# Loading x in half tiles from two queues, and making the edge keys later with one VectorE operation, in a graph attention kernel

## Chip, cores and metric

The kernel runs on one core of a Trainium2 chip. The metric is the device time of one execution in microseconds; lower is better. Where several executions were timed, the median is given.

## What is computed

A graph attention layer on 384 nodes with 1024 features, with a layer norm and a ReLU in front and a residual around it. Everything is float32. Cut to what matters:

```python
h = maximum(layernorm(x), 0)                      # x: [384, 1024]
q = h @ wq.T + bq;  k = h @ wk.T + bk;  v = h @ wv.T + bv
q2 = (q @ wiq.T + biq).reshape(384, 16, 64).transpose(1, 0, 2)      # k2, v2 alike
mask = full((384, 384), -inf)
mask[src, dst] = softplus(edge_type_weights)[edge_type - 1]         # 6528 edges
mask[i, i] = where(mask[i, i] == -inf, softplus(edge_type_weights)[3], mask[i, i])
attn = softmax(q2 @ k2.T * 0.125 + mask)
out = x + (attn @ v2).transpose(1, 0, 2).reshape(384, 1024) @ wo.T + bo
```

Edges can occur twice with different types, and then the last one counts. So the kernel must find out which edges have a later edge with the same cell of the mask.

## The kernel before, in words

**Precision.** Each float32 matrix is split in a high part, which TensorE's float32r format holds, and a low part, the remainder. A product is three matmuls, high by high, high by low and low by high (`mm3`, L367 to L369).

**Stages.** The weights are cut in 56 chunks of 128 x 1024 (512 KB each), in the order v, q, iv, k, iq and ik in turn, o. `load(w)` (L65) asks for chunk w from the queue of SyncE (SP) into one of three buffers `raw`; `split_hi` (L77, on ScalarE) and `split_lo` (L82, on VectorE or GpSimd) make the two parts, in one of four buffers `whl`. The first eight chunks give v from the normalized x, the next eight q, and so on; the attention over 16 heads runs between the chunks of iq and ik and those of o. The order on every engine is written out by hand, so an engine that waits for one instruction holds up all that stands behind it.

**The start**, where the change lies. x is loaded in three tiles `xt[0..2]` of 128 rows (L96). For each tile t:

- `ln_bn` (L251, VectorE, two halves) and `ln_mean` (L254, VectorE; for tiles 0 and 1 also L257 on ScalarE, minus the mean) make mean and variance.
- `ln_sub` subtracts the mean: for tiles 0 and 1 the first 512 columns on ScalarE (L280) and the others on GpSimd (L282), for tile 2 both on VectorE (L284).
- `ln_transpose` (L292, TensorE) turns the tile into two PSUM banks.
- `ln_hi` (L298, ScalarE) and `ln_lo` (L303, VectorE) read them, apply the ReLU, and write the high and the low part of `hT`.

The division by the standard deviation comes later, as a row that multiplies the product (`rrow`, L275), made from `ln_root` on ScalarE and `ln_rstd` on VectorE (L265 to L268).

Chunk 0 of the weights is split by GpSimd, in halves of 512 columns (L344 the high, L346 the low part). Its 24 matmuls (L414) stand in another order than those of the later chunks: eight with high parts alone, four with the low part of the weights, four with the low part of `hT` (k 0 to 3), and again four and four (k 4 to 7). So the low parts of `hT` are wanted in two steps. Chunk 1 is split on ScalarE and, by `split(1, nc.gpsimd)`, on GpSimd.

**The edge keys.** Every edge has a key, 384 times src plus dst. To compare an edge with later ones the kernel needs the keys twice: one edge to a partition (from `ed`), and as rows along the free axis in all partitions. The rows are made so: `er` (128 x 102 integers, 408 bytes a partition: src, then dst) is loaded, `key_rows` turns it into 128 x 51 keys `kr` on GpSimd (L182 to L184) and stores them to `krow` in DRAM (L185, SP), and `key_load` (L205, SP) reads `krow` back, spread over all partitions, into `rows`: three loads of 384 KB for group 0 at the start, others later. `mask_detect` (L217, VectorE) compares, from the end of chunk 0 on.

**Queues at the start.** SP issues, in this order: tile 0 of x, `er`, tiles 1 and 2, chunk 0, `ed`, chunk 1, `bc`, `ew` (small), the store of `krow`, chunk 2, three loads of `rows`, chunk 3. Chunk 3 waits for the buffer of chunk 0. ScalarE's queue issues no transfer there. While x is on its way, TensorE does transposes that nobody reads (`warm`, L309).

Of the kernel before, what the change touches and what calls it, by code (L numbers as in the profile page):

```python
# [12 lines left out]
OP = mybir.AluOpType  # L13

N, D, NT, KT, NP = 384, 1024, 3, 8, 8
E = 6528
EC = E // 128
# [5 lines left out]
def gnn_kernel(ctx: ExitStack, tc: tile.TileContext, x, edges, erows, etw, wq, wk, wv, wiq, wik, wiv, wo,  # L23
# [6 lines left out]
    nc = tc.nc  # L30
# [9 lines left out]
    NTAB, RNG = 3, EC // 3  # L40
# [3 lines left out]
    def bank(tag):  # L44
        return psum.tile([128, 512], F32, tag=tag, name=tag, bufs={"g": 3, "a": 1}.get(tag, 2))
# [14 lines left out]
    def load(w):  # L60
        if w >= NCH:
            return
        n, m = chunks[w]
        raw[w] = wpool.tile([128, D], F32, tag="raw", name="raw", bufs=3)
        nc.sync.dma_start(raw[w], W[n][m])  # L65
# [25 lines left out]
    xt = [xall[:, t * D:(t + 1) * D] for t in range(NT)]  # L91
    xn = [xall[:, (NT + t) * D:(NT + t + 1) * D] for t in range(NT)]
    ert = work.tile([128, N], F32, tag="e", name="er", bufs=EB)
    er = ert[:, :2 * EC].bitcast(I32)
    for t in range(NT):
        nc.sync.dma_start(xt[t], x[t * 128:(t + 1) * 128, :])  # L96
        if t == 0:
            nc.sync.dma_start(er, erows)
    load(0)
    ed = const.tile([128, 3 * EC], I32, name="ed")  # L100
    nc.sync.dma_start(ed, edges)
    load(1)
# [72 lines left out]
            nc.gpsimd.tensor_tensor(val, val, t, OP.add)  # L175

    krt = work.tile([128, N], F32, tag="e", name="kr", bufs=EB)
    kf = ert[:, :2 * EC]

    def key_rows():  # L180

        nc.gpsimd.tensor_copy(kf, er)  # L182
        nc.gpsimd.tensor_scalar(kf[:, :EC], kf[:, :EC], float(N), None, op0=OP.mult)
        nc.gpsimd.tensor_tensor(krt[:, :EC], kf[:, :EC], kf[:, EC:], OP.add)  # L184
        nc.sync.dma_start(krow.rearrange("c j -> (c j)").rearrange("(p e) -> p e", p=128), krt[:, :EC])  # L185

    rows = {}
# [3 lines left out]
    def parts(g):  # L191
        return [(r * RNG + g * PA, min(r * RNG + (g + 1) * PA, (r + 1) * RNG)) for r in range(NTAB)]
# [3 lines left out]
    def key_load(g, s):  # L196

        if s == 0:
            t = work.tile([128, 2, NT, N], F32R, tag="pt", name="rows")
            krv[g] = t.bitcast(F32).rearrange("p a k n -> p (a k n)")  # L200
        c0, c1 = parts(g)[s]
        dst = krv[g][:, s * PA * 128:(s * PA + c1 - c0) * 128]
        for c in range(c0, c1):
            rows[c] = krv[g][:, (s * PA + c - c0) * 128:(s * PA + c - c0 + 1) * 128]
        nc.sync.dma_start(dst, krow[c0:c1, :].rearrange("c j -> (c j)").partition_broadcast(128))  # L205
# [44 lines left out]
    def ln_bn(t, h):  # L250
        nc.vector.bn_stats(lnt[:, 30 + 12 * t + 6 * h:36 + 12 * t + 6 * h], xt[t][:, h * 512:(h + 1) * 512])  # L251
# [25 lines left out]
    def ln_sub(t, c0, c1, eng):  # L277
        src, dst = xt[t][:, c0:c1], xn[t][:, c0:c1]
        if eng is nc.scalar:
            nc.scalar.activation(dst, src, AF.Identity, bias=negm[:, t:t + 1])  # L280
        elif eng is nc.gpsimd:
            nc.gpsimd.tensor_tensor(dst, src, lnt[:, 2 * t:2 * t + 1].to_broadcast([128, c1 - c0]), OP.subtract)  # L282
        else:
            nc.vector.tensor_scalar(dst, src, lnt[:, 2 * t:2 * t + 1], None, op0=OP.subtract)  # L284

    def ln_transpose(t):
        pss = []
        for half in range(2):
            ps = bank("st"[half] if t < 2 else "ga"[half])
            for j in range(4):  # L290
                k = half * 4 + j
                nc.tensor.transpose(ps[:, j * 128:(j + 1) * 128], xn[t][:, k * 128:(k + 1) * 128], ident)  # L292
            pss.append(ps)
        return pss

    def ln_hi(t, half, ps):
        hi = hT[:, 0, half * 4:half * 4 + 4, t * 128:(t + 1) * 128]
        nc.scalar.activation(hi, ps.rearrange("p (k n) -> p k n", k=4), AF.Relu)  # L298
# [7 lines left out]
    def warm(n):  # L306
        for i in range(n):
            ps = bank("g")
            nc.tensor.transpose(ps[:, :128], ident, ident)  # L309

    mask_consts()
    warm(WARM[0])
    key_rows()
    load(2)
    for s in range(NTAB):
        key_load(0, s)
    ln_bn(0, 0)
    ln_bn(0, 1)
    ln_mean(0)
# [13 lines left out]
    ln_mean(2)  # L333
    ln_sub(2, 0, 512, nc.vector)
    ln_sub(2, 512, D, nc.vector)
    p1 = ln_transpose(1)
    warm(WARM[2])
    ln_hi(1, 0, p1[0])
# [6 lines left out]
    for c in (slice(0, 512), slice(512, D)):  # L345
        nc.gpsimd.tensor_tensor(t0[:, 1, c], raw[0][:, c], t0[:, 0, c].bitcast(F32), OP.subtract)  # L346
    load(3)
    ln_hi(2, 0, p2[0])
    ln_hi(2, 1, p2[1])
    ln_root()  # L350
# [416 lines left out]
    for i in range(S + LA + 4):  # L767
        now[0] = i
        r = RATE if len(gens) == 2 else RATE_O if i < S else RATE_E
# [86 lines left out]
```

## Time and profile before

| what | value |
|---|---|
| median of 3 runs | 302.65 us (302.16 to 302.67) |
| the profiled execution | 302.19 us, of which the span of the profile is 300.5 us |
| TensorE (PE) | 293.1 us busy, 98% of the span |
| VectorE (DVE), ScalarE (ACT), GpSimd (POOL) | 200.5, 154.9 and 155.7 us busy |
| DMA | 55.12 MB in 22,377 packets, mean 183 GB/s |
| PE's waits after 12 us | one, of 0.2 us |

How to read it: the profile shows one execution; a time is in us from the start of its span. A line of the timeline gives start, length, engine, line of the kernel, operation, what is written and read, how many instructions are merged, and in brackets the idle time before it with what ended it. `SPq` is the queue on which SP issues transfers; its lines show the issue, not the transfer. Tile names there can stand for several tiles in one buffer: `g` is x, `hT` and the like, and a PSUM bank too.

### The profile page before, as it was taken

What the parts mean: (1) busy time and instruction counts of PE and PEld (TensorE: products, weight loads), DVE (VectorE), ACT (ScalarE), POOL (GpSimd) and SP (SyncE); (2) the same over time, 40 slices, a digit from 0 to 9 for tenths busy, and PEclk for the clock granted to TensorE, in tenths of its full rate; (3) what the DMA queues carried; (4) which work ended last, traced back from release to release, by engine and by line L of the source; (5) the groups of instructions that cost most, each with busy time, mean ns of one, the idle gap of its engine ahead of it and who ended that gap; (6) DMA issues with size and microseconds to landing.
All of it is one profiled execution on the core that took longest, in us unless ns stands there. A gap on an engine that the chain in (4) does not pass through costs nothing.

```text
span 300.5 us, 4961 instructions
## 1 busy us (share of the span) xinstructions
PE 293.1 (98%) x1649; PEld 276.1 (92%) x1649; DVE 200.5 (67%) x492; ACT 154.9 (52%) x289; POOL 155.7 (52%) x164
## 2 busy tenths in 40 slices
PE   7899999999999999999999999999999999999995
PEld 5699999999988889999999999999999998888884
DVE  2959986655956463788865576767576757696523
ACT  3874644333422213554325667777777767676310
POOL 5865766271555785730033737373746467566210
PEclk9999999999999999999999999999999999999999
DMA  7899754642686668475369997646565636910005
GB/s 233 284 297 381 281 164 171 228 143 70 217 238 224 193 217 242 142 274 198 115 169 244 217 221 173 166 127 180 155 170 139 174 81 174 381 41 0 2 0 209
DMA packets 22377, 55.12 MB, mean 183 GB/s; under 512 B 4816, under 2 KB 8400, under 8 KB 22352
## 3 DMA queue, kind: packets, MB, share of 16 engines
q1 hardware_dynamic: 19968, 52.42, 57.7%
q0 software_dynamic: 2064, 1.80, 2.0%
q10 hardware_dynamic: 320, 0.59, 0.8%
q8 instruction: 13, 0.21, 0.3%
q14 instruction: 12, 0.10, 0.1%
HBM read 40.39 MB, written 4.97 MB: 151 GB/s over the span
## 4 chain that ended last, share of the span: by engine, by line
PE 95%; DMA 2%; DVE 1%; ACT 0%; issue 0%; SPq 0%
PE g L369 21%; PE g L367 21%; PE g L368 21%; PE s L694 6%; PE a L731 6%; PE t L714 5%; PE s L369 2%; PE s L368 2%; PE s L367 2%; DMA g<-in_x_dram 2%; PE t L369 2%; PE t L367 2%; PE t L368 2%; PE g L414 1%; PE a L369 1%; PE a L367 1%
## 5 line engine op out<-in xcount | busy, mean ns | idle before, releaser
L367 PE MATMUL g<-g,whl 128*128 128x384 f32 x312 | 106.4, 341 | 0.0
L369 PE MATMUL g<-g,whl 128*128 128x384 f32 x312 | 104.5, 335 | 0.0
L368 PE MATMUL g<-g,whl 128*128 128x384 f32 x312 | 104.2, 334 | 0.0
L228 POOL DMA_INDIRECT tab<-val,idx x51 | 57.6, 1129 | 40.3 <-issue 11.3
L77 ACT ACTIVATE whl<-raw 128x1024 fp32r<-128x1024 f32 x51 | 53.4, 1051 | 31.7 <-PE g L369 20.1
L709 POOL TENSOR_TENSOR e<-e,s 128x384 f32<-128x384 f32 x48 | 39.2, 830 | 41.2 <-DVE s L708 32.9
L368 PEld LDWEIGHTS g<-g,whl 128*128 128x128 f32 x312 | 58.7, 188 | 0.0
L367 PEld LDWEIGHTS g<-g,whl 128*128 128x128 f32 x312 | 58.6, 188 | 0.0
L369 PEld LDWEIGHTS g<-g,whl 128*128 128x128 f32 x312 | 58.5, 188 | 0.0
L82 DVE TENSOR_TENSOR whl<-raw,whl 128x1024 fp32r<-128x1024 f32 x41 | 50.2, 1224 | 9.6 <-ACT whl L77 7.9
L82 POOL TENSOR_TENSOR whl<-raw,whl 128x1024 fp32r<-128x1024 f32 x11 | 26.5, 2412 | 35.6 <-ACT whl L77 31.8
L383 ACT ACTIVATE g<-f,bc 128x384 fp32r<-128x384 f32 x24 | 14.8, 618 | 53.1 <-DVE f L382 46.8
L704 ACT ACTIVATE e<-e,s 128x384 f32<-128x384 f32 x48 | 29.4, 612 | 13.0 <-DVE s L700 13.0
L724 DVE TENSOR_TENSOR pt<-t,pt 128x384 fp32r<-128x384 f32 x48 | 26.4, 550 | 13.9 <-ACT pt L723 13.3
L723 ACT ACTIVATE pt<-t 128x384 fp32r<-128x384 f32 x48 | 23.2, 484 | 13.9 <-PE t L714 13.3
L700 DVE CUSTOM_DVE_ANT_0 e<-s,ma 128x384 f32<-128x384 f32 x48 | 26.3, 550 | 2.0 <-PE s L694 1.8
L694 PE MATMUL s<-ks,qs 128*128 128x384 f32 x96 | 25.3, 344 | 0.3 <-DVE s L700 0.2
L714 PE MATMUL t<-ident,e 128*128 128x128 f32 x144 | 23.5, 271 | 0.0
L382 DVE TENSOR_TENSOR f<-g,rrow 128x384 f32<-128x384 f32 x24 | 13.3, 555 | 13.5 <-PE g L369 7.6
L714 PEld LDWEIGHTS t<-ident,e 128*128 128x128 f32 x144 | 18.8, 140 | 3.1
L378 DVE SCALAR_TENSOR_TENSOR nat<-g,bc,nat 128x384 fp32r<-128x384 f32 x16 | 9.9, 618 | 16.4 <-ACT nat L377 14.4
L731 PE MATMUL a<-pt,vhl 128*128 128x384 f32 x96 | 20.8, 351 | 0.0
(147 smaller groups left out, 414.8 us busy)
## 6 DMA issues: line engine op xcount, KB each, us to landing
ks<-nat SPq DMA_DIRECT2D x30, 192.0 KB
raw<-in_wv_dram SPq DMA_DIRECT2D x8, 512.0 KB
raw<-in_wq_dram SPq DMA_DIRECT2D x8, 512.0 KB
raw<-in_wiv_dram SPq DMA_DIRECT2D x8, 512.0 KB
raw<-in_wk_dram SPq DMA_DIRECT2D x8, 512.0 KB
raw<-in_wiq_dram SPq DMA_DIRECT2D x8, 512.0 KB
raw<-in_wik_dram SPq DMA_DIRECT2D x8, 512.0 KB
raw<-in_wo_dram SPq DMA_DIRECT2D x8, 512.0 KB
```

The costliest lines, as they stand in the source:

```text
L77: nc.scalar.activation(dst[0], raw[w], AF.Copy)
L82: (eng or nc.vector).tensor_tensor(lo, raw[w], hi.bitcast(F32), OP.subtract)
L228: nc.gpsimd.indirect_dma_start(out=tabs[c // RNG], out_offset=bass.IndirectOffsetOnAxis(ap=idx[:, c:c + 1], axis=0), in_=val[:, c:c + 1], ...
L367: nc.tensor.matmul(ps, lhi, rhi, start=first, stop=False)
L368: nc.tensor.matmul(ps, lhi, rlo, start=False, stop=False)
L369: nc.tensor.matmul(ps, llo, rhi, start=False, stop=last)
L694: nc.tensor.matmul(ps[:, :N], qs[:, o, t * 128:(t + 1) * 128], ks[:, o, s, :], start=(s == 0), stop=(s == 1))
L704: nc.scalar.activation(es[i], es[i], AF.Exp, bias=s[:, 0:1], scale=-1.0, accum_out=s[:, 1:2])
L709: nc.gpsimd.tensor_tensor(es[i], es[i], s[:, 2:3].to_broadcast([128, N]), OP.mult)
L714: nc.tensor.transpose(ps[:, k * 128:(k + 1) * 128], es[i][:, k * 128:(k + 1) * 128], ident)
L724: nc.vector.tensor_tensor(lo, pv, hi.bitcast(F32), OP.subtract)
L731: nc.tensor.matmul(ps[:, :N], vhl[:, k, p, 2 * o:2 * o + 2, :], pts[h][:, s, k, :], start=(k == 0 and s == 0), stop=(k == 2 and s == 1))
```

## The change

Each tile of x is loaded in two pieces of 64 rows (256 KB each), the lower from SP's queue and the upper from ScalarE's. `er` is requested behind x and chunk 0 instead of behind tile 0. The keys are made by one VectorE operation (multiply by 384 and add, reading the integers directly) in place of three GpSimd operations. `key_rows`, with its store, stands behind the subtraction of tile 2 on VectorE and behind `load(2)` on SP; the three `key_load`s of group 0 stand behind `load(3)`.

```diff
     for t in range(NT):
-        nc.sync.dma_start(xt[t], x[t * 128:(t + 1) * 128, :])
-        if t == 0:
-            nc.sync.dma_start(er, erows)
+        for q, r in ((nc.sync, 0), (nc.scalar, 64)):
+            q.dma_start(xt[t][r:r + 64, :], x[t * 128 + r:t * 128 + r + 64, :])
     load(0)
+    nc.sync.dma_start(er, erows)
     ed = const.tile([128, 3 * EC], I32, name="ed")
...
     krt = work.tile([128, N], F32, tag="e", name="kr", bufs=EB)
-    kf = ert[:, :2 * EC]
 
     def key_rows():
 
-        nc.gpsimd.tensor_copy(kf, er)
-        nc.gpsimd.tensor_scalar(kf[:, :EC], kf[:, :EC], float(N), None, op0=OP.mult)
-        nc.gpsimd.tensor_tensor(krt[:, :EC], kf[:, :EC], kf[:, EC:], OP.add)
+        nc.vector.scalar_tensor_tensor(krt[:, :EC], er[:, :EC], float(N), er[:, EC:], op0=OP.mult, op1=OP.add)
         nc.sync.dma_start(krow.rearrange("c j -> (c j)").rearrange("(p e) -> p e", p=128), krt[:, :EC])
...
     mask_consts()
     warm(WARM[0])
-    key_rows()
     load(2)
-    for s in range(NTAB):
-        key_load(0, s)
     ln_bn(0, 0)
...
     ln_sub(2, 0, 512, nc.vector)
     ln_sub(2, 512, D, nc.vector)
+    key_rows()
     p1 = ln_transpose(1)
...
     load(3)
+    for s in range(NTAB):
+        key_load(0, s)
     ln_hi(2, 0, p2[0])
```

## The prediction, made before the change was run

> **What bounds the kernel now.** First the share of each engine: PE is busy for 293.1 of 300.5 us. So only a few us can be won without removing matmuls. Then the waits of PE: after 12 us it waits once, for 0.2 us. Then the chain of waits in order of time, from the start to the first weight matmul:
>
> ```profile
> 0.81 0.39 SPq L96
> 1.25 0.42 SPq L98
> 1.72 5.41 DMA g<-in_x_dram
> 7.16 1.30 DVE lnt L251 x2
> 8.96 0.73 ACT g L280
> 9.73 0.66 PE s L292 x4
> 10.39 0.45 PE t L292 x4
> 10.85 0.63 PE g L292 x4
> 11.51 0.66 PE a L292 x4
> 12.26 4.41 PE g L414 x24
> ```
>
> The reader is to see that PE's gapless work begins at 12.26 us, and that one transfer stands in front of it: the second tile of x, asked for at 1.72 us and awaited by VectorE until 7.16. VectorE had finished tile 0 at 5.69 (5.48 + 0.21), so it idled 1.47 us (the timeline says so). A shift of that landing shifts the start of PE, and, as nothing stops PE later, the end.
>
> Why was the tile late? I ask for busy time by stretches (last three columns: clock, DMA share, GB/s):
>
> ```profile
> 3.75:6.00 2.25, 2.21 (x11) 1.55 (x9) 1.50 (x3) 0.24 (x2) 1.19 (x4) 1.00 0.95 245
> 6.00:7.50 1.50, 0.77 (x7) 0.77 (x8) 0.34 (x1) 0.76 (x2) 0.81 (x1) 1.00 1.04 399
> ```
>
> From 3.75 to 6.00 the engines moved 551 KB; at 399 GB/s that takes 1.38 us, so 0.87 us were lost there, just where the 408-byte rows of `er` lie between tiles 0 and 1.
>
> The third view is the timeline of VectorE and GpSimd around the place where the new key operation goes:
>
> ```profile
> 11.14 2.72 POOL L346 TENSOR_TENSOR whl<-raw,whl 128x512 fp32r<-128x512 f32 x2
> 11.38 1.27 DVE L303 SCALAR_TENSOR_TENSOR g<-s,g 128x512 fp32r<-128x512 f32 x2
> ...
> 14.20 2.41 POOL L82 TENSOR_TENSOR whl<-raw,whl 128x1024 fp32r<-128x1024 f32 x1
> 14.37 0.68 DVE L303 SCALAR_TENSOR_TENSOR g<-a,g 128x512 fp32r<-128x512 f32 x1
> 14.96 0.16 DVE L265 RECIPROCAL lnt<-lnt 128x3 f32<-128x3 f32 x1
> 15.23 1.40 DVE L266 TENSOR_TENSOR lnt<-lnt 128x3 f32<-128x3 f32 x1
> 16.58 0.35 POOL L153 TENSOR_SCALAR ed<-ed 128x51 f32<-128x51 f32 x1
> 16.66 0.16 DVE L267 TENSOR_TENSOR lnt<-lnt 128x3 f32<-128x3 f32 x1
> ```
>
> L266 and L267 are alike, three columns each, yet one takes 1.40 us and the other 0.16: L266 ends at 16.63, with GpSimd's L82 (16.61).
>
> **What the Trainium skill says.** "SBUF — State Buffer", Who interferes with whom: a VectorE instruction with two SBUF inputs and a GpSimd instruction that reads SBUF exclude each other; the later one blocks until the earlier ends. L266 agrees (1.40 against 0.16). The new operation has two SBUF inputs; L303, which reads one from PSUM, runs in 0.68 beside L346. "DMA: Bandwidth & Descriptors", Issuing engines are not separate DMA queues: transfers from SP and ACT share the same 16 engines, and a second issuing engine saves issue time only. The trace before doesn't show x from two queues. So I expect nothing from the second queue by itself; SP's issues of x (0.39 to 0.43 us each) all end by 2.62, long before the landings.
>
> **The change part by part.** All times are of the profiled execution.
>
> *er behind x and chunk 0.* It frees tiles 1 and 2 of the 0.87 us at least. VectorE can't start tile 1 before 5.69, so the gain is between 0.87 (landing at 6.29) and 1.47 (5.69 or earlier). Tile 0 landed 3.35 us after its issue (0.81 to 4.16); 512 KB more at 399 GB/s take 1.31 us, which gives 5.47 for tile 1, and 6.8 for tile 2, needed at 7.2. I take a shift of **1.35 us**, nearer the upper end, because the loss in GB/s is a mean and the landing is that of the slowest of 16 engines.
>
> *Pieces of 64 rows, three issues on ACT.* Six issues for three. ACT starts at 0.80 and has a table load (1.28) and a root (0.20) before its first real work at 5.72: 5.72 - 0.80 - 1.50 = 3.4 us are free for three issues. At SP's price they take 1.3 us, hidden. The nearest ACT rows are dearer when both queues issue at once: 0.51 and 0.87 us (L558, L560), up to 2.01 (L567). Ends: a gain of 0.2 (tile 0 a little sooner, my allowance) and a loss of 0.85 us (the third rival). I take nothing.
>
> *SP's order.* In the trace SP's eleventh issue waited 1.3 us for the landing of its third, and its twelfth for that of its fourth; so some issues wait for the one eight before. `ed` may now wait for tile 0 (4.2) where it was issued at 3.14, and chunk 1 follows at 4.6 instead of 3.62. Cover: x, chunk 0 and er are 2.15 MB, on the rings until about 8 us. Chunk 1 is needed at 13.07 - 1.35.
>
> *Three GpSimd operations removed* (0.27, 0.39, 0.29 us). Worth nothing: GpSimd then waited 0.28 us for the mean of tile 0. Its next work (L282, L344, L346, then L82, the low part of chunk 1) hangs on tile 1's mean and on chunk 0, which also loses er ahead of it; L82 ended at 16.61 and PE's L369 read its result from 16.85, a slack of 0.24 that both keep if they move alike.
>
> *One VectorE operation added, after L284 and before the six L303.* The work itself: L223, the same operation on 9 columns, takes 0.17, L217 on 128 columns 0.35; so 0.2 for 51. But at its turn (11.38 less the shift) GpSimd has been in the first half of L346 for 0.24 us, which lasts to about 12.50: a wait of 1.1. Ends: 0.2 (it slips in ahead of L346) and 1.6 (it meets the whole half). I take **1.25** in all. Behind it stand the six L303, pitch 0.6, with the last ending at 15.05; PE needs that one for the last four k of chunk 0, 20 matmuls of 0.177 after the start: 12.26 + 3.54 = 15.80. The slack is 0.75, so PE stalls 1.25 - 0.75 = **0.5 us**. After that L266 waits for L82 anyway, which swallows the rest. The wait for `er` itself costs nothing: chunk 0 lands near 8.3, er soon after, and the turn comes near 10.0.
>
> *The key chain, later.* The store of krow was issued at 5.52 and had landed when SP asked for the rows at 11.82; now it goes out near 11.3, behind chunk 2 (already at about 7), and should land by 13 to 14. Its three row loads (0.33, 0.43, 0.43 us of SP, 1.18 MB) stand behind load(3), which waits for L346 (13.86 less the shift). They can hold up load(4), at 16.64 before, only if krow lands after 14; chunk 4 was split at 24.23, several us of cover. The rows are first read at 23.59 less the shift; chunk 3, queued behind them before, landed 7.0 us after its issue (13.89 to 20.88), so rows asked for at 14 are there by 21. Chunk 3 itself now goes ahead of them. Off PE's path: nothing.
>
> **Sum.** 1.35 - 0.50 = 0.85 us. The profiled execution took 302.19 us (span 300.5 and 1.69 around it): 301.3 by its own measure. It lies 0.46 below the median of the runs, 302.65; against that I predict **301.8 us**.
>
> **Rivals.**
> *No lock.* VectorE's operation gets its turn before L346, since VectorE starts each instruction before the last one ends (11.38 against 10.63 + 0.83). For it: L217 at 23.59 ran in 0.34 beside a GpSimd L174. Against it: L266. The slack of 0.75 then covers it, and the gain is 1.35 to 1.6: 301.2 us.
> *The tile stays late.* The dip after 3.75 is not er's doing, but a trait of the start of the stream. For it: 128 packets of 408 bytes are 52 KB, little by volume. Tile 1 lands near 6.7, a shift of 0.5, eaten by the stall of 0.5: 302.65, no change.
> *ACT as the bound, slower.* ACT's three issues contend with SP's for whatever prepares the transfers (the rows of 0.87 and 2.01 us above). ACT's work on tiles 0 and 1 is one string in program order: mean, subtraction, two evacuations of tile 0, the same of tile 1, then L298 of tile 2. If ACT becomes free at F, the rows of the timeline (0.24 for the mean, 0.72, 0.74 for the transposes, 0.50 and 0.60 for the evacuations, each tile; 0.60 for tile 2) put the start of PE at about F + 6.3. That reaches 12.26 at F = 5.96, so it decides from 1.2 us an issue ((5.96 - 0.80 - 1.50) / 3). At 1.5 us each, F is 6.8, PE starts at 13.1 with VectorE ahead of it, no stall is left, and the time is 302.65 + 0.85 = 303.5 us. Against it: nine SP issues in a row kept a pitch near 0.5 us.
>
> **How the numbers follow.** 0.2%, or 0.6 us, is about what a measurement of this kernel can tell from no change. Forecast with the stall: 0.5, of which 0.4 are beyond 0.6 us and 0.1 (a shift near 1) within. No lock: 0.25, all faster. Tile late: 0.15, within. ACT: 0.1, slower. That makes 0.65, 0.25, 0.10. Range: down to the no-lock case with tile 0 a little sooner (302.65 - 1.65 = 301.0), up past no change to 302.9; the ACT case and the tails are left out.
>
> **What would show it.** Right: the first L251 of tile 1 near 5.7 to 5.9, L414 near 10.9, the key operation taking over 1 us and ending with a half of L346, L414's stage lengthened from 4.24 to about 4.7. No lock: an operation of 0.2 and a stage of 4.24. Tile late: VectorE idle before the second L251. ACT: its L257 of tile 0 after 5.9. I am wrong altogether if L414 starts earlier and PE gains a new wait in the later stages, most likely for chunk 4 or for the key rows.

## The result: slower, against the prediction

The changed kernel takes 305.18 us (median of 6 runs, 304.43 to 305.94), the kernel before 302.59 in the same session: a ratio of 1.0089, 95% interval 1.0069 to 1.0110. I had predicted 301.8, at most 302.9.

The lines of the kernel move a little with the change: the statistics are now L248, the mean L251, the subtraction of tile 2 L281, the transposes L289, GpSimd's split of chunk 0 L339 (high) and L341 (low), the key operation L181, the low parts of `hT` L300, the matmuls of chunk 0 L411.

The chain of waits in order of time of the changed kernel (start, length, what), from the start to the end of chunk 0:

```profile
0.81 0.58 ACTq L97
1.43 0.86 ACTq L97
2.32 8.35 DMA g<-in_x_dram
10.69 1.30 DVE lnt L248 x2
12.01 0.22 DVE lnt L251
12.26 2.33 DVE g L281 x2
14.63 1.12 PE a L289 x4
15.75 4.73 PE g L411 x24
```

The one transfer that stood in front of everything stands there again, and it is longer: the last tile of x, asked for by ScalarE's third issue, is awaited until 10.69. Before, the chain went through tile 1 at 7.16, and tile 2 came into use at 8.61. Chunk 0 ends at 15.75 + 4.73 = 20.48 instead of 12.26 + 4.41 = 16.67: 3.81 us later, of which 3.6 are left at the end (span 304.1 against 300.5; the other 0.2 us come back behind PE's last matmul). The two profiled executions, 305.77 and 302.19 us, lie one above and one below their medians, so the runs show 2.6 us of these 3.6.

The 3.81 us can be read off the chain in three pieces:

- **2.08 us**: tile 2 comes into use later (10.69 against 8.61, where VectorE came to it 0.12 us after its landing).
- **1.05 us** from there to the end of tile 2's subtraction (3.90 us against 2.85). The subtraction itself takes 2.33 instead of 1.34.
- **0.68 us** from there to the end of chunk 0 (5.89 against 5.21).

**The first piece.** Busy time by stretches of the changed kernel (the last three columns: TensorE's clock, DMA share, GB/s):

```profile
4.50:10.70 6.20, 3.27 (x21) 2.46 (x19) 3.00 (x7) 2.56 (x6) 2.06 (x2) 1.00 1.02 256
10.70:13.40 2.70, 1.17 (x9) 0.97 (x10) 2.63 (x5) 1.34 (x3) 1.70 (x4) 1.00 1.09 385
13.40:16.80 3.40, 3.12 (x12) 2.72 (x13) 3.40 (x4) 1.61 (x5) 2.57 (x3) 0.50 0.14 46
```

While the pieces of x move, the 16 DMA engines are busy all the time (1.02) and carry 256 GB/s (228 in its first part, 4.50 to 8.00); as soon as whole chunks of weights follow, the same share carries 385. So it is not that the engines wait for something: each packet takes longer. In the records of single packets, the median of those of 4 KB is 264 ns in the first stretch; before the change it was 159 while x was moving. The pieces also land one after the other, though two queues asked for them in pairs: 4.56 and 5.74 us for tile 0, 6.91 and 8.04 for tile 1, 9.97 and 10.67 for tile 2 (each the last of 16 engines). Whole tiles landed at 4.13, 7.14 and 8.49.

**The second and third piece.** The timeline of the changed kernel:

```profile
11.72 1.17 POOL L339 CAST whl<-raw 128x512 fp32r<-128x512 f32 x2 [1.00 <-DMA raw<-in_wv_dram]
12.26 2.32 DVE L281 TENSOR_SCALAR g<-g,lnt 128x512 f32<-128x512 f32 x2
12.85 2.86 POOL L341 TENSOR_TENSOR whl<-raw,whl 128x512 fp32r<-128x512 f32 x2
14.50 1.28 DVE L181 SCALAR_TENSOR_TENSOR kr<-er 128x51 f32<-128x51 int32 x1
```

Before, the same stretch read:

```profile
8.61 1.23 DVE L251 BATCH_NORM_STATS2 lnt<-g 128x6 f32<-128x512 f32 x2
9.81 1.36 POOL L344 CAST whl<-raw 128x512 fp32r<-128x512 f32 x2
10.12 1.34 DVE L284 TENSOR_SCALAR g<-g,lnt 128x512 f32<-128x512 f32 x2
```

There the second half of the subtraction began (10.63) before the low parts did (11.14), and ended at 11.46, 0.28 us after the last high part (11.18). Now it comes later than GpSimd's work. Its first half ends at 13.18, 0.29 after the last high part (12.89), its second half (13.10 to 14.58) 0.28 after the first low part (12.85 to 14.30). The same 0.28 stands in e1, e2, e3 and e7 below, while a half takes only 0.49 us where it is held up least (e1 and e12, first halves). So a half waits for the operation of GpSimd that is under way when its turn comes, and new in the change is that this is a low part of 1.44 us. The third piece is in the clock column above: from 13.40 to 16.80 TensorE ran at half its clock. The waits of PE up to 21 us say how it got there:

```profile
PE s L289 <- ACT g L277: 3.2, 2, 2.4
PE g L289 <- DVE g L281: 1.2, 1, 1.2
```

PE had too little to do while it waited for late tiles. The key operation took 1.28 us, about the 1.25 foreseen, but PE, at half clock, was then too slow to notice.

### The profile page after: what moved, and what is told of

It reads as the page before. It is cut to its first block, busy times and chain, and to the rows that moved or that the text cites. A ratio compares the mean times of both kernels' runs of the same rounds, so it can differ in the third digit from the quotient of the medians.

```text
span 304.1 us, 4967 instructions
## 1 busy us (share of the span) xinstructions
PE 294.2 (97%) x1649; PEld 277.5 (91%) x1649; DVE 202.7 (67%) x493; ACT 155.0 (51%) x289; POOL 156.6 (52%) x161
## 4 chain that ended last, share of the span: by engine, by line
PE 90%; DMA 5%; DVE 3%; issue 1%; ACTq 0%; ACT 0%; SPq 0%
PE g L366 20%; PE g L364 20%; PE g L365 20%; PE s L691 6%; PE a L728 6%; PE t L711 5%; DMA g<-in_x_dram 3%; DMA raw<-in_wiq_dram 2%; PE s L365 2%; PE s L366 2%; PE s L364 2%; PE g L411 2%; PE t L366 2%; PE t L365 2%; PE t L364 2%; DVE g L281 1%
## 5 line engine op out<-in xcount | busy, mean ns | idle before, releaser
L82 DVE TENSOR_TENSOR whl<-raw,whl 128x1024 fp32r<-128x1024 f32 x41 | 50.3, 1226 | 8.1 <-ACT whl L77 8.1
L82 POOL TENSOR_TENSOR whl<-raw,whl 128x1024 fp32r<-128x1024 f32 x11 | 26.5, 2413 | 36.3 <-ACT whl L77 32.6
```

The source lines that it names most:

```text
L82: (eng or nc.vector).tensor_tensor(lo, raw[w], hi.bitcast(F32), OP.subtract)
```

## The experiments

Theory **H**: 64 rows of a tile move at half the rate of 128, whichever queue asks. Rivals: the second queue or ScalarE's issues; the new place of `er`; the key operation. Twelve kernels were run, in three sessions, each with its own runs of the kernel before (302.63, 302.48 and 302.81 us).

| run | median us | ratio to before, 95% interval |
|---|---|---|
| e1, only the 64-row pieces | 304.39 | 1.0056 (1.0038 to 1.0074) |
| e2, all but the 64-row pieces | 302.23 | 0.9981 (0.9969 to 0.9992) |
| e3, 64-row pieces from SP alone | 304.21 | 1.0051 (1.0031 to 1.0070) |
| e4, pieces of 512 columns, two queues | 302.38 | 0.9990 (0.9973 to 1.0008) |
| e5, e2 with the keys behind the low parts | 304.32 | 1.0048 (1.0025 to 1.0072) |
| e9, e2 with `er` back behind tile 0 | 302.94 | 1.0017 (1.0002 to 1.0032) |
| e7, the change with more warming | 305.17 | 1.0074 (1.0046 to 1.0102) |
| e8, the change, tile 2 on ScalarE | 305.35 | 1.0074 (1.0048 to 1.0099) |
| e12, e7 and e8 together | 304.80 | 1.0062 (1.0038 to 1.0086) |
| e10, the middle rows of x first | 309.08 (one run) | |
| e13, e2 with an operand of the keys in PSUM | 301.72 | 0.9965 (0.9953 to 0.9976) |
| e14, e2 with the keys ahead of the splits | 301.97 | 0.9974 (0.9961 to 0.9986) |

### One part alone, and all but it: e1 and e2

e1 is the kernel before with only this edit:

```diff
-        nc.sync.dma_start(xt[t], x[t * 128:(t + 1) * 128, :])
+        for q, r in ((nc.sync, 0), (nc.scalar, 64)):
+            q.dma_start(xt[t][r:r + 64, :], x[t * 128 + r:t * 128 + r + 64, :])
```

> The kernel before, with x in pieces of 64 rows from two queues and nothing else of the change. Theory H (a piece of 64 rows moves at half the rate of a tile of 128 rows, whatever its queue): tile 2 is complete near 10.7 us instead of 8.5, the subtraction L284 collides with GpSimd's split of chunk 0, TensorE's chunk 0 starts near 15.4 instead of 12.26, and the time is 2.5 to 3.5 us above before (ratio 1.008 to 1.012). Rival O (the later er, the keys and the order of SP cost the time): within 0.5 us of before. Rival A (ScalarE's queue is slow to issue): as H in time, but see e3.

e2 is the change without it:

```diff
-        for q, r in ((nc.sync, 0), (nc.scalar, 64)):
-            q.dma_start(xt[t][r:r + 64, :], x[t * 128 + r:t * 128 + r + 64, :])
+        nc.sync.dma_start(xt[t], x[t * 128:(t + 1) * 128, :])
```

> The change with whole tiles of 128 rows from SP: er behind x and chunk 0, keys by one VectorE operation, the new order. Theory H: the time falls below before by the sum of the prediction without the halves, 0.85 us (0.3 to 1.5; ratio 0.995 to 0.999), tile 1 awaited until 5.5 to 6.3 us, a key operation of over 1 us. Rival O: 2 to 3 us slower than before.

e1 is 1.8 us slower than before, less than the 2.5 to 3.5 that I had put down for H, and e2 is faster than before by 0.0019 of 302.6, some 0.6 us. The stretch from 3.75 to 6.00 us, first of e1, then of e2:

```profile
3.75:6.00 2.25, 1.69 (x11) 1.28 (x9) 0.11 (x1) 0.70 (x2) 0.00 (x0) 1.00 1.04 214
```

```profile
3.75:6.00 2.25, 2.21 (x11) 1.56 (x9) 1.92 (x4) 0.35 (x2) 0.33 (x1) 1.00 0.85 311
```

214 GB/s with engines busy throughout, against 311 with engines that still had idle moments. So the loss is in the pieces, and the rest of the change is a gain. Tile 2 is awaited until 10.80 in e1 and 7.76 in e2.

### Which property of the pieces: e3, e4 and e10

e3 takes the second queue out of the change, e4 keeps both queues and cuts the tile by columns:

```diff
-        for q, r in ((nc.sync, 0), (nc.scalar, 64)):
+        for q, r in ((nc.sync, 0), (nc.sync, 64)):
```

> The change, but both pieces of 64 rows from SP's queue; ScalarE issues nothing. Theory H: as slow as the change, or slower by up to 1 us, since no piece can lie beside another (2.5 to 4 us above before). Rival A (ScalarE's queue): back to the time of before or 0.85 below it. Rival Q (two queues share the 16 engines badly, taking turns): likewise back near before.

```diff
-        for q, r in ((nc.sync, 0), (nc.scalar, 64)):
-            q.dma_start(xt[t][r:r + 64, :], x[t * 128 + r:t * 128 + r + 64, :])
+        for q, c in ((nc.sync, 0), (nc.scalar, 512)):
+            q.dma_start(xt[t][:, c:c + 512], x[t * 128:(t + 1) * 128, c:c + 512])
```

> The change, but the pieces are 512 columns of all 128 rows (256 KB as well, rows of 2 KB), one from SP and one from ScalarE. Theory H: full rate, tile 2 complete by 7.5 us, 0.3 to 1.5 us below before. Rival S (a piece of 256 KB is too small, whatever its shape): as slow as the change. Rivals A and Q: slow as well.

e3 is as slow as e1, with no issue on ScalarE: the loss is there without the second queue. It is less than I had expected, though: 1.6 us above before instead of 2.5 to 4, and some 1.1 us below the change (1.0051 against 1.0089; the intervals just meet, at 1.0070 and 1.0069). So the second queue may have a share in what the change lost; no run separates it. Its six pieces land at 4.43, 5.55, 6.69, 7.87, 9.03 and 10.09, one every 1.06 to 1.18 us, and the stretch reads

```profile
4.50:9.00 4.50, 1.54 (x10) 1.34 (x10) 2.53 (x5) 0.92 (x2) 1.04 (x1) 0.84 1.04 225
```

The profiles also show why the same slow pieces cost the change more. In e1 and e3 the chain to chunk 0 doesn't run through tile 2, but through tile 0, whose second piece lands at 5.86 and 5.55 instead of 4.13, and then through ScalarE's work on tiles 0 and 1; chunk 0 starts at 14.42 and 14.14. The second half of tile 2's subtraction began there before GpSimd's low parts (12.77 against 13.29, 12.24 against 12.75) and was spared the long wait that it had in the change.

e4 has the same two queues, the same six requests of 256 KB, and packets of 2 KB instead of 4, and its median is not distinguishable from before or e2, where I had expected 0.3 to 1.5 us below before. Its profiled execution (304.02 us) is not typical. Four pieces land by 5.47, but those of tile 2 only at 8.10 and 9.49, the last on one engine 1.15 us behind the others, so that VectorE waits:

```profile
9.52 0.69 DVE L248 BATCH_NORM_STATS2 lnt<-g 128x6 f32<-128x512 f32 x1 [0.70 <-DMA g<-in_x_dram]
```

Even so the stretch from 3.75 to 6.00 us has 302 GB/s, against 214 in e1. So neither the size of a request nor the number of queues by itself makes the pieces slow, but the 64 rows.

e10 asks whether it is their number or their place. It requests rows 32 to 95 of the three tiles first, then the outer rows:

```diff
-    for t in range(NT):
-        for q, r in ((nc.sync, 0), (nc.scalar, 64)):
-            q.dma_start(xt[t][r:r + 64, :], x[t * 128 + r:t * 128 + r + 64, :])
+    for r0, r1 in ((32, 96), (0, 32), (96, 128)):
+        for t in range(NT):
+            nc.sync.dma_start(xt[t][r0:r1, :], x[t * 128 + r0:t * 128 + r1, :])
```

The ports of Theory P are those of the page that is named under "Why the prediction was wrong": the doors by which a transfer reaches groups of partitions.

> The change with all of x requested from SP in the order: rows 32 to 95 of tiles 0, 1 and 2, then rows 0 to 31 of the three, then rows 96 to 127. The first three pieces are again 64 rows and 256 KB each, but they lie across the middle of SBUF's partitions instead of at one end. Theory P (a transfer is slow because its partitions reach only half of the ports, as in the two halves of the change): the three middle pieces reach both halves, so they move at the rate of a whole tile, some 380 to 400 GB/s between 2.2 and 4.2 us, in packets of about 160 ns, and the third lands before 4.9 us. Rival S (64 rows are slow as such, whichever they are, or a request of 256 KB is): about 225 GB/s, packets of about 315 ns, the third lands between 5.6 and 6.7 us. In both the 32-row pieces behind them stay slow and the kernel's time is that of the change or longer (304 to 308 us), since no tile is complete before its outer rows are in.

```profile
3.00:4.00 1.00, 1.00 (x6) 0.84 (x6) 0.00 (x0) 0.00 (x0) 0.00 (x0) 1.00 1.13 402
...
7.00:9.50 2.50, 0.00 (x0) 0.00 (x0) 0.00 (x0) 0.00 (x0) 0.00 (x0) 1.00 1.06 220
```

The first two middle pieces land at 3.85 and 4.61, 0.76 us apart where e3's are 1.12 apart; packets that started between 2.5 and 5.5 us have a median of 159 ns, those of the outer rows (7.0 to 9.5) one of 314. It is the place: 64 rows across the middle move in packets as short as those of a whole tile, and the outer rows, 32 at a time, as slowly as the halves. My number for the third piece was missed: ten engines had it by 5.64, the other six by 6.91, while outer rows already moved; why these six fell behind is open. This is one execution, at 309.08 us slower than before, as expected, since no tile is complete before its outer rows are in, but beyond the 304 to 308 that I had put down.

### What the rest is worth: e9 and e5

e9 is e2 with `er` requested behind tile 0, as before the change. e5 is e2 with the key operation, its store and the row loads behind the low parts:

```diff
     for t in range(NT):
         nc.sync.dma_start(xt[t], x[t * 128:(t + 1) * 128, :])
+        if t == 0:
+            nc.sync.dma_start(er, erows)
     load(0)
-    nc.sync.dma_start(er, erows)
```

> e2 with er behind tile 0 again, as before; keys as in the change. Theory R (er between tiles 0 and 1 costs tiles 1 and 2 and chunk 0 about 0.7 us): tile 1 is awaited until about 7 us and the time is 0.4 to 0.8 us above e2, so 0 to 0.4 us above before, the stall of the key operation being left. Rival D (the dip in the stream of x comes at that time whatever lies there): as e2 within 0.2 us.

```diff
     ln_sub(2, 512, D, nc.vector)
-    key_rows()
...
     load(3)
-    for s in range(NTAB):
-        key_load(0, s)
...
     ln_lo(2, 1, p2[1])
+    key_rows()
+    for s in range(NTAB):
+        key_load(0, s)
```

> Whole tiles and er behind chunk 0, as in e2, with the key operation (and its store and the three row loads) moved behind the six L303 operations on VectorE. Theory L (in e2 the key operation waited 1.1 us for GpSimd's L346 and so held up the low parts that TensorE wants): chunk 0's 24 matmuls take 4.24 us again instead of 4.71, and the time falls by 0.3 to 0.5 us below that of e2 (ratio to before 0.996 to 0.998). Rival: the wait only moves, to GpSimd's L82 and the standard deviation behind it, or the later row loads hold up chunk 4: the time of e2 or more.

Between e9 and e2 lies 0.0036 of the time, 1.1 us: that is the worth of `er`'s place, in two sessions and with intervals of about 0.0015 each. It is more than the 0.4 to 0.8 that I had expected. In the profiles tile 2 lands at 8.82 in e9 and at 7.74 in e2, and chunk 1 starts at 17.46 and 16.43. e9 itself is not below before: it has the key operation on VectorE without `er`'s gain, and chunk 0 takes 4.84 us instead of 4.24.

e5 was a miss. I expected the stall to go, and it went, but some 2 us (1.0048 against e2's 0.9981) were lost elsewhere. Its timeline:

```profile
13.98 2.40 POOL L82 TENSOR_TENSOR whl<-raw,whl 128x1024 fp32r<-128x1024 f32 x1
...
14.75 1.71 DVE L180 SCALAR_TENSOR_TENSOR kr<-er 128x51 f32<-128x51 int32 x1
...
19.92 1.28 SPq L201 DMA_DIRECT2D rows<-krow  x3
21.29 0.38 SPq L65 DMA_DIRECT2D raw<-in_wv_dram  x1
```

The keys wait for another low part of GpSimd's (L82, to 16.38). Their store was issued at 16.48 and landed on 15 engines by 17.96, on the last at 19.90. Until then SP could issue neither the row loads nor chunk 4 (the last line), which landed at 28.9, and PE waited for it. This is the case that the prediction named ("only if krow lands after 14"). In the change the store landed at 17.35, but everything there is later, and PE doesn't wait for chunk 4.

### Where the rest of the 3.8 us lies: e7, e8 and e12

```diff
-    WARM = (20, 6, 0)
+    WARM = (30, 10, 6)
```

> The change with more of the transposes that nobody reads: 30, 10 and 6 instead of 20, 6 and 0. Theory C (TensorE idled so much while x arrived that its clock was halved from 13.4 to 16.8 us, which cost the first four matmuls of chunk 0 0.7 us): clock 1.0 to the end, chunk 0 in 4.24 us plus what the low parts then hold up, time 0.3 to 0.7 us below the change (ratio to before 1.006 to 1.008). Rival: the landing of x alone sets the time, and nothing changes (1.0089).

```diff
-    ln_sub(2, 512, D, nc.vector)
...
     ln_hi(1, 1, p1[1])
+    nc.scalar.mul(negm[:, 2:3], lnt[:, 4:5], -1.0)
+    ln_sub(2, 512, D, nc.scalar)
```

> The change, with the second half of the subtraction of tile 2 on ScalarE instead of VectorE. Theory B (of the 3.8 us that the change lost, 1.0 came from L281 waiting on VectorE for GpSimd's split of chunk 0): that half ends near 13.6 instead of 14.58, TensorE's chunk 0 starts 0.5 to 0.9 us earlier, and so does the end (ratio to before 1.006 to 1.008). Rival: the transfers alone set the start, no change.

e12 has both edits.

> The change with more warming transposes (30, 10, 6 in place of 20, 6, 0) so that TensorE's clock stays granted, and the second half of tile 2's subtraction on ScalarE instead of VectorE, so that it can't wait for GpSimd's split. Theory B (what the late tile costs beyond its own delay is the wait of the subtraction behind GpSimd, about 0.97 us, and the halved clock, about 0.67 us, both gone here): chunk 0 starts at about 14.3 us or earlier instead of 15.75, its stage takes 4.3 to 4.9 us at a clock of 1.0, chunk 1 starts at 18.5 to 19.0 instead of 20.32, and the ratio is 1.002 to 1.005, near that of the 64-row pieces alone (1.0056). Rival (the rest is lost elsewhere, so that these two cover it only in the trace): the ratio stays at 1.007 or above.

In e7 the clock stays full, and the stall of the low parts comes back at once, as the chain shows, with the key operation and the six low parts between the subtraction and the matmuls:

```profile
12.03 2.29 DVE g L281 x2
14.32 1.21 DVE kr L181
15.53 3.60 DVE g L300 x6
```

So the half clock and the stall cover each other; taking one away brings 0.3 us in the profile (chunk 1 at 19.98 instead of 20.32) and nothing that the runs can tell: the median of e7, with a mean clock of 0.998 or more in all six executions, is 305.17 us, that of the change 305.18, with 0.989 to 0.994 in five of six; its sixth, at 1.000, is the slowest (305.94). e8 alone is inconclusive. In its profile the second half of the subtraction ends at 14.43, hardly before the change's 14.58, because on ScalarE it stands behind other work; and the clock was half for 10.24 us:

```profile
9.40:19.70 10.30, 9.27 (x36) 8.01 (x34) 9.45 (x15) 8.04 (x15) 7.19 (x7) 0.50 0.79 265
```

In e12 the clock is full, the half of the subtraction left on VectorE takes 0.49, and chunk 1 starts at 18.56, as expected, 2.06 us later than before. That this is so near the 2.08 of the first piece is chance. Tile 2 landed at 9.86 here and was hardly awaited; the chain runs through tile 0, awaited until 5.62 instead of 4.16, and then through ScalarE's work, up to its half of tile 2:

```profile
5.62 1.30 DVE lnt L248 x2
12.78 0.73 ACT g L277
14.21 4.52 PE g L412 x24
```

So the slow pieces cost about 2 us even without the other two, but by the first tile, not the last. The median of e12 is 2.0 us above before. I had expected a ratio of 1.002 to 1.005 and measured 1.0062, between that and the rival's 1.007. Against the change (1.0089) the intervals still overlap: that the second and third piece cost time is shown in the traces, and in the runs only made likely.

### Better versions: e13 and e14

e13 copies one operand of the keys to PSUM (`pe`, which is `ps` in `key_rows`), in a gap of ScalarE:

```diff
     ln_sub(1, 0, 512, nc.scalar)
+    pe = bank("g")
+    nc.scalar.activation(pe[:, :EC], er[:, EC:], AF.Copy)
...
-        nc.vector.scalar_tensor_tensor(krt[:, :EC], er[:, :EC], float(N), er[:, EC:], op0=OP.mult, op1=OP.add)
+        nc.vector.scalar_tensor_tensor(krt[:, :EC], er[:, :EC], float(N), ps[:, :EC], op0=OP.mult, op1=OP.add)
...
-    key_rows()
+    key_rows(pe)
```

> The change with whole 128-row tiles from SP (e2), and the second operand of the key operation brought into a PSUM bank by a ScalarE copy of 51 columns, in ScalarE's gap behind its half of tile 1's subtraction. The key operation then has one input in SBUF and one in PSUM. Theory L (the 1.28 us of the key operation are 1.1 us of waiting for GpSimd's low part, because both its inputs lie in SBUF, and some 0.2 us of work): it takes 0.15 to 0.35 us here, while GpSimd's L341 runs beside it; the low parts on VectorE start 0.9 us earlier, chunk 0's stage is 4.2 to 4.3 us instead of 4.71, and the kernel is 0.2 to 0.5 us faster than e2: ratio 0.9960 to 0.9977. Rival (the 1.28 us are the work itself, or the conversion from integers): still about 1.2 us, and the ratio stays at 0.998.

e14 makes the keys before GpSimd has a split to do:

```diff
+    nc.sync.dma_start(er, erows)
     load(0)
-    nc.sync.dma_start(er, erows)
...
     ln_bn(2, 1)
+    key_rows()
     ln_mean(2)
     ln_sub(2, 0, 512, nc.vector)
     ln_sub(2, 512, D, nc.vector)
-    key_rows()
```

> The change with whole 128-row tiles from SP (e2), the edge rows requested behind x but ahead of the first weight chunk, and the key operation placed on VectorE right behind the statistics of tile 2, before its subtraction, when GpSimd has no split to do yet. Theory L: the key operation takes about 0.2 us (nothing of GpSimd's runs beside it), the keys are stored near 9.5 us instead of 12, and the stall of the low parts goes; the first weight chunk lands up to 1 us later behind the narrow rows of the edge rows, which GpSimd's split of chunk 0 feels: chunk 0 starts between 11.5 and 12.6 us and the ratio is 0.996 to 1.0005. Rival (the key operation is 1.2 us of work wherever it stands): tile 2's subtraction and chunk 0 come 1.2 us later, and the ratio is 1.001 or above.

The timelines, e13 (with GpSimd's low parts beside it), then e14:

```profile
10.10 2.71 POOL L342 TENSOR_TENSOR whl<-raw,whl 128x512 fp32r<-128x512 f32 x2
...
10.34 0.20 DVE L180 SCALAR_TENSOR_TENSOR kr<-er,g 128x51 f32<-128x51 int32 x1
```

```profile
9.38 0.20 DVE L180 SCALAR_TENSOR_TENSOR kr<-er 128x51 f32<-128x51 int32 x1
```

The operation is 0.2 us of work in both; the other 1.1 us were a wait for GpSimd. In e13 it runs in the middle of GpSimd's low part, with one operand in PSUM. In both, chunk 0's stage is back at about 4.25 us. e13 has the lowest median here: 1.1 us below before (0.0035 of 302.8) and, by the two ratios (1.0089 and 0.9965), some 3.8 us below the change. The intervals of e13, e14 and e2 overlap, so the runs don't rank the three.

## Why the prediction was wrong, step by step

**The step that failed is "Pieces of 64 rows, three issues on ACT", with "I take nothing".** I weighed the issues and the queue, and not the rows. The rate of a piece was neither in my sum nor among its ends. 256 KB took 1.1 to 1.2 us where 512 KB had taken about 1.2 (e3, e2). In the change tile 2 comes into use 2.1 us later by it, and with that comes the rest: the late tile 2 meets GpSimd's low parts, and PE starves until its clock is halved. The pieces alone cost 1.8 us in the runs (e1), of 2.6 for the whole change. The Trainium skill states it, on a page that I had used for something else: "SBUF — State Buffer", Door 1: The DMA port swizzle (why `[64,N]` ≈ `[32,N]`), says that partitions 0 to 63 reach only 8 of the 16 ports, with a limit of about 218 GB/s. The trace agrees in the main: 214 GB/s in e1, 225 in e3, 220 for e10's outer rows. The 256 of the change lie above the limit; the first 3.5 us of that stretch have 228, and behind them the last two pieces seem to move together (the fifth lands 1.93 us behind the fourth, the sixth 0.70 behind the fifth). e10 also agrees with the page's table, by which rows 32 to 95 reach both halves. The same page, "Can I just issue two DMAs to hit both halves?", says that two such transfers serialize; the first four pieces of the change, asked for in pairs and landing 1.1 to 1.2 us apart, are that. Where it says that only a transfer over all 128 partitions hits all ports, e10's middle rows (402 GB/s between 3.00 and 4.00) show otherwise.

**er behind x: right in kind, too large in size.** I took a shift of 1.35 us. e2's chunk 0 starts 0.54 us earlier than before. Tile 1 landed at 5.26, even better than the 5.47 foreseen, but tile 2 at 7.74 instead of 6.8, and so it became the one that is awaited. Of the 0.87 us that I had counted as lost between 3.75 and 6.00, e2 still loses (399 - 311) × 2.25 / 399 = 0.50. The rival "the tile stays late" had that half of it right. In e2 tile 2 landed on the first engine at 6.46 and on the last 1.28 us after; why some engines fall behind there is open. With x in halves the gain is gone: tile 2 is awaited to 10.80 in e1, with `er` in between, and to 10.69 in the change.

**The key operation: right.** 1.25 us foreseen, 1.28 and 1.27 measured in the change and e2, and split as I had split it, 0.2 of work and 1.1 of waiting (e13, e14). What I left out is that tile 2's subtraction, which I took as fixed, waits for GpSimd too. "SBUF — State Buffer", Who interferes with whom, on which I leaned for this, holds. The "no lock" rival is excluded.

**The stall of 0.5 us: right where it could show.** In e2 the chain runs through it, and chunk 0's stage takes 4.71 instead of 4.24:

```profile
9.33 1.45 DVE g L280 x2
10.78 1.20 DVE kr L180
11.98 3.60 DVE g L299 x6
15.62 0.97 PE g L410 x4
```

**The key chain, later: right.** After chunk 0 PE waits twice for 0.2 us in the change, both times in the attention stage (once before the change), and never for chunk 4 or the keys; e5 shows how much later is too late.

**SP's order, and GpSimd's three operations.** `ed` did wait for tile 0 (issued at 5.75), and chunk 1 followed at 6.13; it landed at 13.39, before anything wanted it. That removing GpSimd's operations is worth nothing was tested by no run alone.

**ACT as the bound: the right sign by the wrong mechanism.** I let it decide from 1.2 us an issue. The three issues took 2.13 us together, ScalarE was free at 4.47 and first needed at 7.32, and e3 loses as much as e1 without them. The sign that I had named for it, the mean of tile 0 after 5.9 us, came (7.32), but because tile 0 landed at 5.74. One part of it was right: ScalarE's work on tiles 0 and 1 is one string, and in e1, e3 and e12 it is the path to chunk 0, started late by a late tile 0.

**The sum.** Without the pieces I would have owed 0.85 us; e2 gained 0.6 (0.2 to 0.9). That it came so near is luck. At chunk 1 the profile of e2 is only 0.07 us ahead of before (16.43 against 16.50), a shift of 0.54 and a stall of 0.47. Some 0.4 us more come in the attention stage, between 161 and 179 us, for which the prediction had no step. e3, e5, e9, e13 and e14 gain 0.4 to 0.6 there too (so of e13's 0.9 us in the profile only 0.34 are won at the start), e1, e4 and the change gain nothing, e7 loses 0.7; why is open.

## What to carry to other kernels

When a tile is cut for a transfer, cut it by columns, so that each piece still spans all 128 partitions (here even that brought nothing that the runs can tell: e4 against e2); a busy DMA share with low GB/s and packets of twice the usual length is the sign of a piece that doesn't. Price what a transfer's shape does to its rate before the price of its issue. Ask which work of another engine a late tile will now meet. And where VectorE has a small operation with two SBUF inputs, place it where GpSimd is idle, or bring one input in through PSUM.

## What the runs showed of the hardware that I had not expected

- A half tile of 64 rows at either end of the partitions moves at about 225 GB/s and holds all 16 DMA engines busy meanwhile (225 and a share of 1.04 in e3); 64 rows across the middle had packets of 159 ns, like a whole tile.
- A subtraction with a column as its scalar, float32 from SBUF to SBUF (L281), waits for GpSimd too: its second half took 1.48 us in the change, 0.83 before, and a half took 0.49 where it was least held up. "SBUF — State Buffer", Who interferes with whom, says of this kind of operation that it can take both ports; the trace agrees.
- TensorE's clock was granted in stretches of 3.41 us. It fell to half after stretches in which PE had been busy for 0.92, 1.10, 1.21 and 1.32 us (e1, e3, e8, the change), and did not after 1.65 and 1.93 (the change, before). That is not the whole rule: in e8 it stayed at half after 2.82 and 2.97, where in e3 it rose after 2.77. The record begins with the first switch, and the clock column shows 1.00 before it; there transposes took 0.42 us, as at half clock, instead of 0.27. "TensorE: Matmul & The Clock Gate", What's actually happening, has this window; here it was not idle, only too little used.
- A store of 25.5 KB landed on 15 DMA engines within 1.5 us and on the last 1.9 us later (e5), and what waits for it waits for that one.
